# Layer 0's logits in seven tiles of 128 tokens for every eight image columns, the eighth column's weights put together by transfers

## The chip, the cores and the metric

The kernel runs on one core of a Trainium2 chip. A core has five engines that run side by side: TensorE (PE, matmuls; PEld is its weight load), VectorE (DVE), ScalarE (ACT), GpSimd (POOL) and SyncE (SP, which here only issues transfers). ACT and POOL issue transfers too. The metric is the device time of one execution in microseconds (us), and the median of several is given.

## The reference, cut to what matters

Two layers of "outlook" attention on images of 56 x 56 pixels with 384 channels, batch 8. Each layer normalises its input over groups of channels and adds its result to it. In layer 0 every pixel gets, for each of 12 heads, a 9 x 9 matrix of weights (a softmax over its last index) from its own normalised channels. These weights mix the values of its 3 x 3 neighbourhood, and the nine results are added back to the nine pixels.

```python
def _L0_conv_ref(x, Wv, Wa, Wo):             # x is normalised: _gn(x)
    v = jnp.einsum('bhwc,oc->bhwo', x, Wv)
    ...                                       # v_unf: the 3 x 3 neighbourhood of v
    a = jnp.einsum('bhwc,oc->bhwo', x, Wa).reshape(b, n, heads, k2, k2)
    attn = jax.nn.softmax(a * d ** (-0.5), axis=-1)
    out = jnp.einsum('bnhpq,bnqhd->bnphd', attn, v_unf).reshape(b, h, w, k2, c)
    ...                                       # canvas: out[..., p] added to neighbour p
    return jnp.einsum('bhwc,oc->bhwo', y, Wo)

x = x + _L0_conv_ref(_gn(x), L0_conv_Wv, L0_conv_Wa, L0_conv_Wo)
x = x + _L1_conv_ref(_gn(x), ...)             # layer 1: not touched by the change
```

## The kernel before, in words

Images go in pairs. A **column** is one image column of a pair: 2 x 56 = 112 tokens (`R`), so a pair has 56 columns (`W`) and the four pairs have 224. Layer 0 is one loop over **steps** 0 to 226 (line 802); step s attends to column s and carries older columns on behind it, so that each engine has work from several columns:

- `attend` (561): for each of three row offsets, three matmuls (`project`, each recorded twice on PE) give 288 logits for the column's 112 tokens in one of three banks of PSUM that are used in turn. DVE takes the maximum and subtracts it into the tile `at`, ACT takes the exponential. The weights of the logits are `wa_t`, the normalised input is `xn`. In seven of eight columns a tile of 128 tokens, taken across column borders, is also projected to values (`pv`, `wv_t`); ACT copies it to `v` and its queue stores it into the DRAM table `vtab0` (`spread`, 316).
- one step later `normalise` (589): DVE sums and inverts, POOL multiplies `at` by `den`.
- two steps later `presum` (602): POOL adds the weights of a column and its two neighbours into `pre`.
- three steps later `fold` (632): ACT and a small matmul with `shift` (`pw`) move rows, DVE adds into a weight tile `wt`, and ACT's queue stores it into the DRAM table `ztab0`. The weight tiles are zeroed in part by POOL before they are used again (`weights_of`, 509).

Seven columns make a **group** (`px`; seven is `PX`). Ten and eleven steps after its first column a group is loaded back: `fetch_v` (675) loads two tiles `vp` of values, `fetch` (683) two tiles `z` of weights and the residual `xres`, all on SP's queue. Four jobs `contract` (matmuls `pc`, which ACT copies to `yT`) and six jobs `project_out` (matmuls `po`, to which DVE adds `xres`) follow; they are queued with a due step, four steps after `fetch`. A step that attends has four gaps, `between(0)` to `between(3)` (813), which place the other work between its matmuls. Jobs run in gaps 0 and 2.

```python
            def between(n):

                if n == 0:
                    next(turning, None)
                    weigh()
                    jobs.run(step, 1)
                elif n == 1:
                    next(folding, None)
                    next(turning, None)
                elif n == 2:
                    jobs.run(step, 1)
                else:
                    next(folding, None)
```

So of seven steps five have jobs (remainders 1 to 5 by seven) and two have none (6 and 0). `weigh` calls `normalise` and `presum`.

The next pair's input is transposed in between (`turned`, 790), and its column blocks of four are loaded (`load`, 542) and normalised (`normed`, 550) into `xn`, which holds eight columns. `upkeep` (760) stores blocks of the first pair and fills borders of the tables with zeros, on SP's queue. The order on PE, DVE and ACT is the program's; some instructions of POOL and SP are placed by the scheduler, near their place in the program. A transfer of SP's or ACT's queue is issued in the order of its engine, so one that waits holds back what that engine has behind it.

Of the kernel before, what the change touches and what calls it, by code (L numbers as in the profile page):

```python
# [15 lines left out]
def two_outlook_layers(  # L16
# [167 lines left out]

    PH_ALL = K * HEADS0
    inside = const.tile([R, K, PH_ALL], F32, name="inside")
    gpsimd.memset(inside, 1.0)
    for b in range(IMG):
        for pi, row in ((0, b * H), (2, b * H + H - 1)):
            gpsimd.affine_select(  # L190
                out=inside[:, pi, :], in_=inside[:, pi, :], compare_op=ALU.not_equal, fill=0.0,
                base=-row, pattern=[[0, PH_ALL]], channel_multiplier=1,
            )

# [120 lines left out]

    def spread(queue, table, width, col, pad, row, v):
# [5 lines left out]
        queue.dma_start(  # L322
            bass.AP(
                table.tensor, table.offset + first,
                [[line, rows], [(R + GAP) * line - PX * C, n], [1, C]],
            ),
            v.unsqueeze(1).to_broadcast([rows, n, C]),
        )
# [73 lines left out]
    def layer0(late, pools):  # L402
# [15 lines left out]
        def xr_tile(pair, blk):  # L418
            return io.tile([P, XB, C], F32, tag="xr", name=f"xr_{pair}_{blk}")[:R]

        def stats_chunk(pair, blk, i):

            if blk == 0 and i == 0:
                stats[pair] = stat.tile([P, NCH, IMG, NBLK, 6], F32, tag="st0", name=f"st0_{pair}")
            if i == 0 and pair:
                xts[pair, blk] = block_tile("xt", pair, blk)
            xr, xt = xrs[pair, blk], xts[pair, blk]
            if pair == 0:
                pt = bank(P, 0, XB * R).rearrange("p (m r) -> p m r", m=XB)
# [12 lines left out]
            yield  # L442
# [11 lines left out]
        def blocks_in(flat, n, at=0):  # L454
# [11 lines left out]
        homes = [  # L466
            block_tile("xin", 0, 0),
            block_tile("xin", 0, 1),
            block_tile("xt", 0, 2),
            block_tile("xt", 0, 3),  # L470
            *blocks_in(first_vp[0], 2),
            *blocks_in(z_flat[1], 3),
            *blocks_in(z_flat[0], 1, NCH * NA0),
# [29 lines left out]

        wts = [fixed.tile([R, E0, HEADS0, PX], F32, name=f"wt0_{n}") for n in range(PX)]
        for wt in wts:
            vector.memset(wt, 0.0)
        held = [(0, 0)] * PX

        def weights_of(sx):

            f0, f1 = max(0, E0 - 1 - sx), min(E0, SX0 - sx)
            m0, m1 = f0 + sx - E0 + 1, f1 + sx - E0 + 1
            n = (*range(PX), 2, 3, 0, 1)[sx]
            wt = wts[n].rearrange("r e h m -> r e m h")
# [5 lines left out]
            return wts[n], wt[:, :, m0:m1, :], f0, f1  # L520

        xn = fixed.tile([P, NCH, SB, R], F32, name="xn0")

# [18 lines left out]
        def load(g):  # L542
            pair, blk = divmod(g, NBLK)
            xins[g] = io.tile([P, NCH, XB, R], F32, tag="xin", name=f"xin_{g}")
# [5 lines left out]
        def normed(g, chunks):  # L550
            scale, bias = params[g // NBLK]
            xin, to = xins[g], xn[:, :, g % 2 * XB : (g % 2 + 1) * XB, :]
            for i in chunks:
                for b in range(IMG):
                    rows = slice(b * H, (b + 1) * H)
                    scalar.activation(
                        to[:, i, :, rows], xin[:, i, :, rows], AF.Identity,
                        bias=bias[:, i, b : b + 1], scale=scale[:, i, b : b + 1],
                    )

        def attend(pair, c, between):

            nm = f"0_{pair}_{c}"
            lhs = xn[:, :, c % SB, :]
            at = work.tile([R, K, K2, PH], F32, tag="at", name=f"at_{nm}", bufs=4)
            mx = work.tile([R, K, PH], F32, tag="mx", name=f"mx_{nm}", bufs=1)
            for pi in range(K):
                pl = bank(R, BANK - NP0, BANK)
# [3 lines left out]
                vector.tensor_tensor(  # L572
                    at[:, pi], pl, mx[:, pi, :].unsqueeze(1).to_broadcast([R, K2, PH]), ALU.subtract
                )
                between(pi)
            scalar.activation(at, at, AF.Exp, scale=SCALE0)
            attns[pair, c] = at
            if c % SB:
                tile_no = c % SB - 1
                tokens = xn.rearrange("p i m r -> p i (m r)")[:, :, tile_no * P : (tile_no + 1) * P]  # L580
                pv = bank(P, 0, C)
                project(pv, tokens, wv_t, 0, C)
                v = work.tile([P, C], F32, tag="v", name=f"v_{nm}")
                scalar.copy(v, pv)
                for lo, m, row, n in parts_of(tile_no):
                    spread(scalar, vtab0, SX0, c - c % SB + m, 2, row, v[lo : lo + n])
            between(K)

        def normalise(pair, c):

            nm, at = f"0_{pair}_{c}", attns[pair, c]
            d4 = work.tile([R, K, 4, PH], F32, tag="d4", name=f"d4_{nm}", bufs=1)
# [3 lines left out]
            den = work.tile([R, K, PH], F32, tag="den", name=f"den_{nm}", bufs=1)  # L596
            vector.tensor_add(den, d4[:, :, 0], at[:, :, 8])
            vector.reciprocal(den, den)
            vector.tensor_mul(den, den, inside)
            nc.gpsimd.tensor_tensor(at, at, den.unsqueeze(2).to_broadcast([R, K, K2, PH]), ALU.mult)  # L600

        def presum(pair, c):
# [4 lines left out]
            def of(t, f, n):  # L607

                a = attns.get((pair, c + t))
                if a is None:  # L610
                    return None
                a = a.rearrange("r pi (qi qj) (pj h) -> r (pi qi) qj pj h", qj=K, pj=K)
                return a[:, :, 1 - t, f - 1 - t : f - 1 - t + n, :]
# [18 lines left out]
        def fold(pair, c):  # L632
# [5 lines left out]
            for px, sx in patches_of(c, 2):  # L638
                wt, to, f0, f1 = weights_of(sx)
                for e, pi, qi in ((0, 0, 2), (E0 - 1, 2, 0)):  # L640
                    scalar.activation(
                        to[:, e], pre[:, pi, qi, f0:f1, :], AF.Copy, scale=inside[:, qi, 0:1]
                    )
# [116 lines left out]
        def upkeep(step):  # L760

            pair, c = divmod(step, W)
            if pair == 0:

                for n in (2 * step, 2 * step + 1):
                    if n < NBLK:
                        keep_block(0, n ^ 2 if n < 4 else n)
                if c == 3:
# [14 lines left out]
            g, j = divmod(step + 2 * XB, XB)  # L783
            if j == 0 and 1 < g < NPAIR * NBLK:
                load(g)
            g, j = divmod(step + XB, XB)
            if j < NCH and g < NPAIR * NBLK:
                normed(g, (j,))

        def turned(step):  # L790
# [7 lines left out]
        vector.on = scalar.on = True  # L798
        xins.update({blk: homes[blk] for blk in range(2)})
        normed(0, range(NCH))  # L800
        LAG = 3
        for step in range(NPAIR * W + LAG):
# [3 lines left out]
            def weigh():  # L806

                if 1 <= step < NPAIR * W + 1:
                    normalise(*divmod(step - 1, W))
                if 2 <= step < NPAIR * W + 2:  # L810
                    presum(*divmod(step - 2, W))

            def between(n):
# [10 lines left out]
                else:  # L824
                    next(folding, None)

            if step < NPAIR * W:
# [346 lines left out]
```

## Time and profile before

| | |
|---|---|
| median of three runs | 3492.05 us (3486.11 to 3503.93) |
| the profiled execution: time, span | 3492.61 us, 3490.9 us |
| mean granted TensorE clock | 0.973 |
| layer 0's loop, from its first logits to its last | 62 to about 2260 us |
| logits of layer 0 on PE | 4032 matmul records, 1101.8 us busy |
| DMA, mean over the span | 240 GB/s |
| SP's queue (q1), ACT's queue (q10), POOL's (q0): share of 16 DMA engines | 48.2%, 21.2%, 7.6% |

A group of the profile is read as: line, engine, operation, what it writes and reads with the tiles' names, count, then busy time, mean nanoseconds of one, and the idle time of the engine just before, with what ended it. A "releaser" is what ended a wait. Windows give busy time of each engine between two moments, the granted clock (1.00 is full) and the share of the DMA engines that was busy. Line 118 is the helper of all matmuls, line 133 that of most other instructions.

### The profile page before, as it was taken

To read this page: it belongs to the slowest core of one execution; us is meant where nothing else is said; L and a number is where in the kernel's file an instruction comes from. 1 tells how busy PE (TensorE), PEld (TensorE's weight loads), DVE (VectorE), ACT (ScalarE), POOL (GpSimd) and SP (SyncE) were. 2 spreads that over 40 slices of the span, in tenths; PEclk is the share of its full clock that TensorE was granted. 3 is DMA by queue.
4 is the path that set the end of the run, shared out by engine and by line. 5 is a ranking of instruction groups with operands and counts; after the bars stand their busy time and mean duration, and the time that the engine had idled before them with its cause. 6 is when DMAs were issued, how large, how long until landed. Compare 5 with 4: busy or idle time off the path is not lost.

```text
span 3490.9 us, 74006 instructions
## 1 busy us (share of the span) xinstructions
PE 3315.4 (95%) x29014; PEld 2233.6 (64%) x29014; DVE 1977.1 (57%) x4797; ACT 1276.5 (37%) x3175; POOL 1258.3 (36%) x2069
## 2 busy tenths in 40 slices
PE   7897999999999999999999999978999999999997
PEld 5565666666666666666666666645666666666665
DVE  6675676767776777677777767632333323333331
ACT  4333333333333333333333333323343434343432
POOL 2543444444444444444444444522222212222220
PEclk8999999999999999999999999989999999999999
DMA  7898876868886877887766776767787787878875
GB/s 244 260 316 269 264 264 225 284 227 266 271 289 228 265 240 255 272 268 251 249 215 214 265 226 229 250 224 205 215 226 219 219 224 213 237 217 227 227 213 145
DMA packets 603259, 839.51 MB, mean 240 GB/s; under 512 B 194910, under 2 KB 496926, under 8 KB 598814
## 3 DMA queue, kind: packets, MB, share of 16 engines
q1 hardware_dynamic: 321662, 537.49, 48.2%
q10 hardware_dynamic: 253984, 210.56, 21.2%
q0 software_dynamic: 27264, 86.73, 7.6%
q8 instruction: 228, 3.74, 0.5%
q14 instruction: 121, 0.99, 0.1%
HBM read 512.95 MB, written 321.69 MB: 239 GB/s over the span
## 4 chain that ended last, share of the span: by engine, by line
PE 70%; DMA 15%; DVE 5%; issue 3%; ACT 3%; ACTq 3%; POOL 0%; SPq 0%; DVEq 0%; POOLq 0%
PE bank L118 38%; PE po L118 17%; PE pc L118 8%; DMA z<-ztab 4%; ACTq L133 3%; PE pw L118 3%; DMA at<-lgtab 2%; DMA xres<-xT 2%; DMA lgtab<-lgt 2%; ACT xn L133 2%; PE pt L121 2%; DMA ztab<-wt 1%; PE bank L121 1%; DVE mx L133 1%; DMA ztab<-zeros 1%
## 5 line engine op out<-in xcount | busy, mean ns | idle before, releaser
L118 PE MATMUL bank<-wa_t,xn 128*112 128x288 f32 x4032 | 1101.8, 411 | 13.2 <-ACT xn L133 6.6
L600 POOL TENSOR_TENSOR at<-at,den 112x972 f32<-112x972 f32 x224 | 504.4, 2252 | 1193.1 <-DVE den L133 1051.9
L118 PEld LDWEIGHTS bank<-wa_t,xn 128*112 128x112 f32 x4032 | 691.8, 178 | 297.1 <-issue 32.0
L118 PE MATMUL po<-yT,wo_t 128*128 128x448 f32 (+1 forms) x2304 | 816.4, 494 | 5.6 <-DVE x1t L133 5.1
L118 PEld LDWEIGHTS po<-yT,wo_t 128*128 128x128 f32 x2304 | 427.8, 190 | 286.9 <-issue 183.8
L133 DVE TENSOR_REDUCE mx<-bank 112x36 f32<-112x324 f32 x672 | 324.9, 484 | 431.8 <-PE bank L118 429.6
L322 POOL DMA_DIRECT2D vtab<-v x392 | 213.1, 547 | 833.1 <-DVE v L133 820.5
L133 ACT ACTIVATE at<-at 112x972 f32<-112x972 f32 (+1 forms) x256 | 243.9, 953 | 669.0 <-DVE at L133 668.9
L118 PE MATMUL bank<-wc_t,xn 128*128 128x438 f32 x1176 | 480.1, 545 | 5.7 <-issue 5.7
L118 PE MATMUL pc<-z,vp 121*32 121x49 f32 (+1 forms) x17664 | 379.9, 220 | 88.2 <-ACT yT L133 66.9
L118 PEld LDWEIGHTS pc<-z,vp 121*32 121x32 f32 (+1 forms) x17664 | 342.5, 122 | 158.2 <-ACT yT L133 88.6
L118 PE MATMUL bank<-wv_t,xn 128*128 128x384 f32 x1176 | 434.5, 507 | 0.0
L133 ACT ACTIVATE xn<-xin,bias,scale 128x224 f32<-128x224 f32 x336 | 174.1, 566 | 515.0 <-DMA ztab<-wt 210.4
L133 DVE TENSOR_TENSOR at<-bank,mx 112x324 f32<-112x324 f32 x672 | 333.0, 496 | 38.2
L118 PEld LDWEIGHTS bank<-wc_t,xn 128*128 128x128 f32 x1176 | 215.2, 192 | 176.5 <-issue 169.9
L118 PEld LDWEIGHTS bank<-wv_t,xn 128*128 128x128 f32 x1176 | 227.0, 197 | 142.4 <-issue 22.4
L622 POOL TENSOR_TENSOR pre<-at,at 112x108 f32<-112x108 f32 (+1 forms) x440 | 236.2, 537 | 58.6 <-ACT wt L133 35.9
L133 ACT COPY yT<-pc 128x294 f32<-128x294 f32 (+2 forms) x512 | 194.8, 405 | 169.8 <-PE pc L118 155.3
L133 DVE TENSOR_TENSOR lgt<-bank,ba_t 128x54 f32<-128x54 f32 x196 | 41.7, 213 | 354.5 <-PE bank L118 346.2
L133 DVE SCALAR_TENSOR_TENSOR x1t<-po,bo_t,x1t 128x448 f32<-128x448 f32 (+1 forms) x156 | 97.6, 626 | 247.3 <-PE po L118 247.3
L133 DVE RECIPROCAL den<-den 112x108 f32<-112x108 f32 (+1 forms) x256 | 198.8, 777 | 8.8
L133 ACT COPY ot<-pt 112x384 f32<-112x384 f32 x128 | 61.3, 479 | 382.4 <-PE pt L121 360.1
(106 smaller groups left out, 2913.8 us busy)
## 6 DMA issues: line engine op xcount, KB each, us to landing
z<-ztab SPq DMA_DIRECT2D x64, 2352.0 KB
vp<-vtab SPq DMA_DIRECT2D x64, 1536.0 KB
vp<-vtab SPq DMA_DIRECT2D x64, 945.0 KB
xres<-xT SPq DMA_DIRECT2D x32, 1176.0 KB
ztab<-wt ACTq DMA_DIRECT2D x336, 110.2 KB
xin<-xT ACTq DMA_DIRECT2D x54, 672.0 KB
z<-ztab SPq DMA_DIRECT2D x128, 258.4 KB
x1t<-x SPq DMA_DIRECT2D x26, 1176.0 KB
```

Source lines behind the costliest of these rows:

```text
L118: tc.keep_in_program_order(nc.tensor.matmul(*args, **kwargs))
L121: tc.keep_in_program_order(nc.tensor.transpose(*args, **kwargs))
L133: return lambda *args, **kwargs: tc.keep_in_program_order(op(*args, **kwargs))
L322: queue.dma_start(bass.AP(table.tensor, table.offset + first, [[line, rows], [(R + GAP) * line - PX * C, n], [1, C]],), v.unsqueeze(1).to_ ...
L600: nc.gpsimd.tensor_tensor(at, at, den.unsqueeze(2).to_broadcast([R, K, K2, PH]), ALU.mult)
L622: nc.gpsimd.tensor_tensor(dst, terms[0], terms[1], ALU.add)
```

## The change

The unit of `attend` becomes a tile of 128 tokens: one column (112 tokens) and 16 rows, eight of each image, of the eighth column of its group of eight (an **eighth** below). Seven such tiles cover eight columns. In the step of the eighth column (7 mod 8, a **short step** below) `attend` does nothing but call the gaps. `xn` becomes two buffers of seven tiles, normalised eight columns ahead; the odd block's last column is normalised in pieces of eight rows.

`share_out` makes the eighth column's weights, on SP's queue: the 16 rows of tiles 0 to 4 are written to the DRAM buffer `last` as each is ready; in the short step 80 rows are read back from it, and the 16 rows of tiles 5 and 6 are copied from tile to tile. `presum` and `fold` then use the result as they used a column before. The values of the 16 rows are stored with a transfer of their own. There are four weight tiles `wts` instead of seven, one buffer of `xin` instead of two, and a third job in a short step.

The core of the diff:

```diff
+    lasts = [dram.tile([R, NA0], F32, name=f"last_{n}") for n in range(2)]
+    NTILE = SB - 1
+    PART = H // NTILE
...
-        wts = [fixed.tile([R, E0, HEADS0, PX], F32, name=f"wt0_{n}") for n in range(PX)]
+        NWT = 4
+        wts = fixed.tile([P, NWT, E0 * HEADS0 * PX], F32, name="wts0")
+        xns = [fixed.tile([P, NCH, NTILE, P], F32, name=f"xn0_{n}") for n in range(2)]
...
-            n = (*range(PX), 2, 3, 0, 1)[sx]
+            n = (0, 1, 2, 3, 0, 1, 3, 2, 3, 0, 1)[sx]
...
         def attend(pair, c, between):
-            lhs = xn[:, :, c % SB, :]
-            at = work.tile([R, K, K2, PH], F32, tag="at", name=f"at_{nm}", bufs=4)
+            k, j = divmod(c, SB)
+            if j == NTILE:
+                for n in range(K + 1):
+                    between(n)
+                return
+            lhs = xns[(pair * W // SB + k) % 2][:, :, j, :]
+            at = work.tile([P, K, K2, PH], F32, tag="at", name=f"at_{nm}", bufs=4)
...
-            if c % SB:
-                tile_no = c % SB - 1
...
-                for lo, m, row, n in parts_of(tile_no):
-                    spread(scalar, vtab0, SX0, c - c % SB + m, 2, row, v[lo : lo + n])
+            spread(scalar, vtab0, SX0, c, 2, 0, v[:R])
+            end = c - j + NTILE
+            if len([*patches_of(end, 2)]) == 1:
+                spread(scalar, vtab0, SX0, end, 2, j * PART, v[R:], ((H, IMG), (1, PART)))
+            else:
+                for b in range(IMG):
+                    lo = R + b * PART
+                    spread(scalar, vtab0, SX0, end, 2, b * H + j * PART, v[lo : lo + PART])
...
+        def share_out(pair, c):
+            k, j = divmod(c, SB)
+            at, last = attns[pair, c], lasts[(pair * W // SB + k) % 2]
+            if j < NTILE - 2:
+                sync.dma_start(
+                    bass.AP(
+                        last.tensor, last.offset + j * PART * NA0,
+                        [[H * NA0, IMG], [NA0, PART], [1, NA0]],
+                    ),
+                    at[R:].rearrange("p a b c -> p (a b c)"),
+                )
+                return
+            whole = work.tile([P, K, K2, PH], F32, tag="at", name=f"at_0_{pair}_{c + 1}", bufs=4)
+            attns[pair, c + 1] = whole
+            for b in range(IMG):
+                n = b * H + (j - 1) * PART
+                sync.dma_start(
+                    whole[b * H : n].rearrange("p a b c -> p (a b c)"), last[b * H : n]
+                )
+            for t in (1, 0):
+                for b in range(IMG):
+                    n, lo = b * H + (j - t) * PART, R + b * PART
+                    sync.dma_start(whole[n : n + PART], attns[pair, c - t][lo : lo + PART])
...
             def weigh():
-                if 1 <= step < NPAIR * W + 1:
+                if 1 <= step < NPAIR * W + 1 and (step - 1) % SB < NTILE:
                     normalise(*divmod(step - 1, W))
                 if 2 <= step < NPAIR * W + 2:
+                    if (step - 2) % SB < NTILE - 2:
+                        share_out(*divmod(step - 2, W))
                     presum(*divmod(step - 2, W))
+                if step < NPAIR * W and step % SB == NTILE:
+                    share_out(*divmod(step - 1, W))
...
                 else:
                     next(folding, None)
+                    if step % SB == NTILE:
+                        jobs.run(step, 1)
```

In `load` and `normed` the buffer count and the split change as told above; in `upkeep` the calls come four columns earlier.

More of the change, by code (lines that the diff above doesn't have):

```diff
@@ L182, in two_outlook_layers, with outside @@
         gpsimd.memset(shift[:, 0, b * H - 1 : b * H], 0.0)
-    PH_ALL = K * HEADS0
-    inside = const.tile([R, K, PH_ALL], F32, name="inside")
+    NTILE = SB - 1
+    PART = H // NTILE
+    inside = const.tile([P, NTILE, K], F32, name="inside")
     gpsimd.memset(inside, 1.0)
-    for b in range(IMG):
[L189 to L193, printed above, removed]
+    def outside(j, pi, partition):
+        it = inside[:, j, pi : pi + 1]
+        gpsimd.affine_select(
+            out=it, in_=it, compare_op=ALU.not_equal, fill=0.0,
+            base=-partition, pattern=[[0, 1]], channel_multiplier=1,
+        )
+    for b in range(IMG):
+        for j in range(NTILE):
+            outside(j, 0, b * H)
+            outside(j, 2, b * H + H - 1)
+        outside(0, 0, R + b * PART)
+        outside(NTILE - 1, 2, R + b * PART + PART - 1)
     NZERO = (EP0 - E0) * ROW0
@@ L314, in parts_of, with spread @@
         yield R - done, tile_no + 1, 0, done + OVER
-    def spread(queue, table, width, col, pad, row, v):
+    def spread(queue, table, width, col, pad, row, v, rows_of=None):
         (px, sx), *more = patches_of(col, pad)
@@ L519, in weights_of @@
             held[n] = m0, m1
-            return wts[n], wt[:, :, m0:m1, :], f0, f1
-        xn = fixed.tile([P, NCH, SB, R], F32, name="xn0")
+            return weights, wt[:, :, m0:m1, :], f0, f1
         wa_t = fixed.tile([P, NCH, K * NL], F32, name="wa0_t")
@@ L587, in attend @@
-            between(K)
+            pv = bank(P, 0, C)
+            project(pv, lhs, wv_t, 0, C)
+            v = work.tile([P, C], F32, tag="v", name=f"v_{nm}")
+            scalar.copy(v, pv)
+            spread(scalar, vtab0, SX0, c, 2, 0, v[:R])
[6 more added lines that the diff above has]
+                    spread(scalar, vtab0, SX0, end, 2, b * H + j * PART, v[lo : lo + PART])
@@ L783, in upkeep @@
             g, j = divmod(step + 2 * XB, XB)
-            if j == 0 and 1 < g < NPAIR * NBLK:
-                load(g)
-            g, j = divmod(step + XB, XB)
             if j < NCH and g < NPAIR * NBLK:
                 normed(g, (j,))
+            if step < NCH:
+                normed(1, (step,), shared=False)
+            if j == NCH - 1 and 2 < g + 1 < NPAIR * NBLK and g > 2:
+                load(g + 1)
         def turned(step):
@@ L798, in layer0 @@
         vector.on = scalar.on = True
-        xins.update({blk: homes[blk] for blk in range(2)})
+        xins.update({blk: homes[blk] for blk in range(4)})
         normed(0, range(NCH))
+        normed(1, range(NCH), whole=False)
         LAG = 3
```

76 lines of the change are left out of this document (43 added, 33 removed).

## The prediction

> **What bounds the kernel now.** I read the page first: busy shares, the chain, the costliest group.
>
> ```profile
> PE 3315.4 (95%) x29014; PEld 2233.6 (64%) x29014; DVE 1977.1 (57%) x4797; ACT 1276.5 (37%) x3175; POOL 1258.3 (36%) x2069
> PE 70%; DMA 15%; DVE 5%; issue 3%; ACT 3%; ACTq 3%; POOL 0%; SPq 0%; DVEq 0%; POOLq 0%
> L118 PE MATMUL bank<-wa_t,xn 128*112 128x288 f32 x4032 | 1101.8, 411 | 13.2 <-ACT xn L133 6.6
> ```
>
> PE sets the pace, and layer 0's logits are a third of its work. But 15% of the chain is DMA, so I went on to the chain in order of time (start, us, what):
>
> ```profile
> 1032.41 18.69 DMA xres<-xT
> ...
> 1169.23 4.84 PE bank L118 x18
> ...
> 1514.52 20.22 DMA z<-ztab
> ...
> 1589.42 19.76 DMA xres<-xT
> ```
>
> One column's logits, 18 records, cost PE 4.84 us. The loads of z take 20 us. The 1.2 MB of xres take 19 us, because they are issued some 5 us after z on SP's queue and are served after it. Next SP's timeline and the windows for step 103, the kind of step that matters below:
>
> ```profile
> 1095.84 0.99 SPq L334 DMA_DIRECT2D z<-ztab  x2
> 1102.11 0.58 SPq L718 DMA_DIRECT2D xres<-xT  x1
> ```
>
> ```profile
> core 0: us, PE busy (x) PEld busy (x) DVE busy (x) ACT busy (x) POOL busy (x), PEclk, DMA share, GB/s
> 1106.00:1115.00 9.00, 6.73 (x29) 4.41 (x28) 6.88 (x18) 4.25 (x6) 3.13 (x4) 1.00 1.05 401
> 1115.00:1122.00 7.00, 6.84 (x116) 4.72 (x118) 6.01 (x15) 2.95 (x6) 5.06 (x8) 1.00 0.54 164
> 1052.40:1054.90 2.50, 0.48 (x39) 0.48 (x43) 0.80 (x3) 2.29 (x7) 2.42 (x6) 1.00 0.85 299
> 1054.90:1058.30 3.40, 3.40 (x77) 2.42 (x66) 0.77 (x2) 2.25 (x7) 1.02 (x3) 0.50 0.05 15
> ```
>
> The burst (z twice, then xres) holds the 16 DMA engines full until 1115, 19 us after its issue; by the xres row of 1032.41, whose z was issued at 1027.19, it lasts 24. The last two rows: 2 us without matmuls, then 3.4 us at half clock. Idle PE time thus costs more than itself. Two prices more, POOL's timeline of one column and the landing of a small transfer:
>
> ```profile
> 1098.64 2.25 POOL L600 TENSOR_TENSOR at<-at,den 112x972 f32<-112x972 f32 x1 [7.38 <-DVE den L133]
> 1100.97 0.41 POOL L622 TENSOR_TENSOR pre<-at,at 112x108 f32<-112x108 f32 x1
> ...
> 1102.52 0.28 POOL L620 COPY pre<-at 112x108 f32<-112x108 f32 x1
> ```
>
> ```profile
> vtab<-v POOLq DMA_DIRECT2D x56, 48.0 KB, 4.1
> ```
>
> **What goes.** Every eighth column has no logits: 28 x 4.84 = 135.5 us of PE. 128 tokens instead of 112 cost nothing: the moving side stays 288, and the values' projection, with 128 on its fixed side, takes no longer per moving column (six of 384 in 2.10 us against six of 288 in 1.62 on PE's timeline). The values' projections keep number and shape. DVE, ACT and POOL lose the softmax of 28 columns; they are not the bound, so that counts at nothing.
>
> **What moves, with nothing on the path.** Normalising x runs eight columns ahead, not four, and splits the odd block: 168 more ACTIVATEs, each under the 0.51 us of the 168-element row, against 28 exponentials of 0.95 us saved; ACT is at 37%. The load of x gets one buffer and about two steps (18 us), an eighth early; a 672 KB transfer lands in some 8 us by the chain's rows for xT (7.77, 8.45). Four weight tiles for seven raise the POOL memsets of weights from 236 to 327 (compiled order), 0.41 us each, on an engine at 36%; without that cover they would cost 91 x 0.41 = 37 us at most.
>
> **What is added.** The eighth column's weights exist only after SP has written 16 rows of tiles 0 to 4 to DRAM, read 80 rows back and copied 16 rows each of tiles 5 and 6. The compiled order shows where these stand: in the short step (7 mod 8), on SP's queue, in program order with z, vp and xres. Behind the assembly wait POOL's sum for column 6, then PE's shift of column 6 (`pw`) in the second step after, and everything PE has after that; DVE too, since the next column's buffer is the one column 5 leaves.
>
> z of a group of seven columns is issued at the start of steps 5 mod 7, and the short step passes through all seven phases. Two are bad.
>
> *Phase 5 (steps 47, 103, 159, 215):* z and xres are queued just before the assembly. With step 103's start, 1092.9, as zero: burst over at 22, transfers landed at 26 (4.1, the row above), POOL's first four sums 2 us: 28. PE meanwhile has two projections and, in three of four pairs, the matmuls of the norm (6 to 7 us), a step without jobs (three times 1.62, 2.1 for the values, 0.57: 7.5) and two thirds of the logits (3.2): it stands at 16.5. Wait 12 us, four times: 48. Ends: 0 if the queue is quicker than I read, 17 with the burst of 24 us.
>
> *Phase 6 (55, 111, 167):* z was issued one step earlier (1165.48, burst over near 1184, 13 us into step 111), but the write of tile 4's rows is queued behind it too, and the read waits for that write: 13 + 4 + 4 + 2 = 23. PE has 0.6 us in the short step, 7.5 and 5.3 in the next two, and some 3 us of wait for column 5, whose exponential, normalising (3.1 on DVE) and 2.25 on POOL lose the cover of a whole column: 16.5. Waits 3 + 6.5, three times: 28. Ends 0 and 16 each.
>
> After each of these seven waits PE runs 3.4 us or twice that at half clock and loses half of it: 7 x 2.5 = 18.
>
> *Other short steps.* Jobs that stood between logits now follow each other: in phases 3 and 4 output projections share one bank, so each waits for DVE's 0.62 us add and its start (1.5 us a step, 8 steps); phase 2 waits for ACT's copies of yT, phase 0 for column 5's chain (1.5 each, 4 steps each): 24 us, between 0 and 40.
>
> *First image pair.* The zero fills of the tables are on SP's queue too (one row of the chain is a fill of 17.55 us at 116.93; SP spends 19.43 us from 197.00 on issuing one set). Short steps 7, 15 and 23 stand behind one each: 10 + 14 + 8 = 32, between 5 and 45.
>
> *End.* Step 223's assembly stands behind the last burst but one, with nothing after it to hide it: 8, between 0 and 15.
>
> *Queue slots.* In the compiled order SP's and ACT's transfers share eight completion counters, and one waits for the transfer that had the counter before. An eighth issues 66 transfers, not 52, so ACT meets z's counter two steps after it, not three: ACT blocks earlier, while the burst sets when it goes on. ACT waits for such transfers now for 190.6 us between 300 and 2250 at its xn instructions alone, and most of that is hidden. I take 15, between -20 (its stalls merge with the seven) and 60.
>
> A page speaks against the small transfers: the Trainium skill, "DMA: Bandwidth & Descriptors", section "Why a DMA increments its semaphore by 16 and not by 1", says that a transfer is spread over the largest number of engines up to 16 that divides the slowest dimension of both sides. The write of two images by eight rows would then use two engines, its reads of 40 rows ten. No run here shows it; by it the last term would lie near its upper end and the sum near 3575, an estimate from that page. For the change speaks the Trainium skill, "Trainium Kernel Development and Optimization", "Best Practices", to tile to 128 partitions always; by that alone the sum would be 3490.9 - 135.5 = 3355.
>
> **Sum,** against the profiled execution's span: 3490.9 - 135.5 + 48 + 28 + 18 + 24 + 32 + 8 + 15 = 3528. That execution took 3492.61 for its span of 3490.9, 0.02% over the median of 3492.05, so 3530.
>
> **Rivals.** *The assembly arrives in time.* In five of seven phases nothing large is queued. If the small transfers overtook the burst, the two bad phases and their clock loss (94) would shrink to about 10, and half of the fills' term would go: 3530 - 84 - 16 = 3430, faster. It decides from a landing within 14 us of the short step's start. Against it: xres and the stores of x, issued during a burst, landed after it.
>
> *Only the long waits are real.* The small terms (24, 32, 8, 15) come to a half, 40, as jobs and logits swap places without loss: 3491, no change.
>
> *ACT falls behind.* Counters and crowded engines hold ACT past the burst, so that yT comes late in every group of seven (by the list of waits PE and its weight loads wait for ACT's yT 95 times already): 2 us more in each of 32 groups: 3594.
>
> That the change doesn't remove the work is excluded: the compiled order has seven sets of nine logits' matmuls for every eight columns.
>
> **How the numbers follow.** Forecast 0.39 (3530, by itself 3512 to 3560), in time 0.22, only the long waits 0.22, ACT behind 0.17. A difference within 0.5% (17 us) is about what a measurement of this kernel can tell from none. Faster by more is the first rival, 0.22; within 0.5% the second, 0.22; slower the forecast and the third, 0.56. The range takes both outer cases and little more: 3425 to 3600.
>
> **What would show it.** Right: `bank<-wa_t,xn` at 3528 records and some 964 us; PE gaps of about 12 us before `pw` in the second step after steps 47, 103, 159, 215, released by POOL `pre`, with SP's reads of `last` landing after xres; half clock after each. Wrong: no gap over 5 us there (first rival), or most of PE's new idle time in front of `pc` with ACT's yT as releaser (third). A PE busy time that does not fall by some 130 us would upset the first term.

## The result, and the profile after

The changed kernel takes 3746.04 us (median of four, 3740.01 to 3756.74) against 3494.16 for the kernel before in the same comparison: a ratio of 1.0723, 95% interval 1.0686 to 1.0760. The forecast was 3530, its range ended at 3600. The direction was right and the size was not.

From the page of the changed kernel: the busy line, the chain by engine, and two groups (busy, mean ns of one, idle before and what ended it).

```profile
PE 3288.0 (88%) x28510; PEld 2241.7 (60%) x28510; DVE 1837.8 (49%) x4454; ACT 1300.7 (35%) x3315; POOL 1222.6 (33%) x2160
PE 35%; DMA 9%; issue 3%; DVE 2%; ACT 2%; POOL 1%; ACTq 0%; SPq 0%; POOLq 0%; DVEq 0%
L119 PE MATMUL bank<-wa_t,xn 128*128 128x288 f32 x3528 | 999.3, 422 | 40.8 <-ACT xn L134 36.9
L119 PE MATMUL bank<-wv_t,xn 128*128 128x384 f32 x1176 | 453.0, 525 | 97.3 <-DVE at L134 97.3
```

PE fell from 95% to 88% busy. The chain accounts for little over half of the span here, so its 35% of PE can't be set beside the 70% of before; I went by the waits. The logits have the 3528 records that were foretold, but cost 422 ns each, not 411. Only 27 us of PE's 3315 went, where one eighth of the logits is 137.7: most of the rest came back as work at half clock (mean granted clock 0.931, before 0.973). The values' projection, which waited for nothing before, now waits 97 us for DVE.

The matmul records give an account of the loop of layer 0, from the first `pw` to the last, with PE's gaps over 0.15 us:

| | before | after |
|---|---|---|
| ahead of the loop | 84.3 | 90.1 |
| loop, matmuls | 2094.8 | 2062.3 |
| loop, gaps | 94.6 (51 of them) | 368.5 (102) |
| behind the loop | 1216.9 | 1223.9 |

Without the 137.7 us the matmuls would take 1957.1; they took 105 us more. By the record of the clock, matmul time at half clock in the loop is 255 us after and 87 before; half of the difference, 84 of the 105 us, is lost by it. With 274 us of new gaps and 13 us at the two ends, less the 137.7, this makes the 254 us between the spans.

The changed kernel's list of waits says where PE and DVE stop (who waits for whom, us, times, longest):

```profile
DVE at L134 <- DMA last<-at: 148.1, 19, 12.6
PE bank L119 <- DVE at L134: 100.0, 15, 9.9
PE pc L119 <- ACT yT L134: 97.0, 40, 11.7
PE pw L119 <- POOL pre L677: 73.4, 10, 14.9
```

Two timelines show two of these waits. First SP in step 103 and PE in step 105, where a long wait was foretold, with the windows around it (columns as in the windows of the prediction):

```profile
1218.92 2.90 SPq L134 DMA_DIRECT2D at<-last  x2
1222.67 10.63 SPq L134 DMA_DIRECT2D at<-at  x4
```

```profile
1236.34 1.14 PE L119 MATMUL pw<-pre,shift 112*112 112x120 f32 x4 [9.03 <-POOL pre L677]
```

```profile
1227.30:1236.30 9.00, 0.01 (x1) 0.00 (x0) 2.50 (x6) 0.00 (x0) 1.14 (x4) 0.64 0.77 292
1236.30:1239.70 3.40, 3.36 (x10) 2.65 (x11) 1.92 (x5) 1.57 (x4) 2.72 (x3) 0.50 0.24 59
```

SP needs 10.63 us to get the four copies out; POOL's sum and `pw` follow. PE does nothing for 9 us (first row of the windows: 0.01 us of PE) and then runs 3.4 us at half clock (0.50). In the compiled order the first of these copies takes the completion counter that a load of z had, and the last the one that xres had: SP issues them only when those have landed (at 1222.61 and 1232.65 in the trace). Second, step 77 (PE):

```profile
922.04 1.63 PE L119 MATMUL bank<-wa_t,xn 128*128 128x288 f32 x6
933.25 3.69 PE L119 MATMUL bank<-wv_t,xn 128*128 128x384 f32 x6 [9.58 <-DVE at L134]
```

No assembly stands here. An early write of 16 rows, issued at 921.26 after z (906.73) and xres (912.14, itself held until 918.6) on SP's queue, lands at 932.58, when they are through: the last packet of xres starts at 931.2, and those of the write run from 930.5 to 931.9. Until then its tile `at` is not free, DVE can't subtract into it, and PE has no bank. The prediction priced these writes at nothing.

### The profile page after: what moved, and what is told of

Read it like the earlier page. It is cut to its first block, busy times and chain, and to the rows that moved or that the text cites. A ratio compares the mean times of both kernels' runs of the same rounds, so it can differ in the third digit from the quotient of the medians.

```text
span 3745.1 us, 73661 instructions
## 1 busy us (share of the span) xinstructions
PE 3288.0 (88%) x28510; PEld 2241.7 (60%) x28510; DVE 1837.8 (49%) x4454; ACT 1300.7 (35%) x3315; POOL 1222.6 (33%) x2160
## 3 DMA queue, kind: packets, MB, share of 16 engines
q1 hardware_dynamic: 328774, 558.40, 46.8%
## 4 chain that ended last, share of the span: by engine, by line
PE 35%; DMA 9%; issue 3%; DVE 2%; ACT 2%; POOL 1%; ACTq 0%; SPq 0%; POOLq 0%; DVEq 0%
PE bank L119 17%; PE po L119 10%; PE pc L119 5%; DMA at<-lgtab 2%; DMA lgtab<-lgt 2%; PE pw L119 1%; DMA z<-ztab 1%; ACT xn L134 1%; DMA last<-at 1%; DMA vtab<-v 1%; PE pt L122 1%; PE bank L122 1%; DMA xres<-xT 1%; DVE den L134 0%; DVE mx L134 0%
## 5 line engine op out<-in xcount | busy, mean ns | idle before, releaser
L119 PE MATMUL bank<-wa_t,xn 128*128 128x288 f32 x3528 | 999.3, 422 | 40.8 <-ACT xn L134 36.9
L119 PE MATMUL po<-yT,wo_t 128*128 128x448 f32 (+1 forms) x2304 | 836.4, 503 | 40.3 <-DVE x1t L134 37.7
L119 PEld LDWEIGHTS bank<-wa_t,xn 128*128 128x128 f32 x3528 | 672.7, 198 | 265.8 <-ACT xn L134 34.0
L134 POOL TENSOR_TENSOR at<-at,den 128x972 f32<-128x972 f32 x196 | 441.2, 2251 | 1122.9 <-DVE den L134 658.2
L134 DVE TENSOR_REDUCE mx<-bank 128x36 f32<-128x324 f32 x588 | 285.7, 486 | 447.3 <-PE bank L119 444.8
L134 ACT ACTIVATE at<-at 128x972 f32<-128x972 f32 (+1 forms) x228 | 215.5, 945 | 645.5 <-DVE at L134 645.4
L134 ACT ACTIVATE xn<-xin,bias,scale 128x168 f32<-128x168 f32 (+1 forms) x474 | 208.3, 502 | 621.8 <-DMA ztab<-wts 261.9
L134 DVE TENSOR_TENSOR at<-bank,mx 128x324 f32<-128x324 f32 x588 | 291.5, 496 | 222.9 <-DMA last<-at 148.1
L134 ACT ACTIVATE wts<-pre,inside 112x48 f32<-112x48 f32 (+4 forms) x672 | 180.1, 359 | 83.1 <-POOL wts L134 18.2
L119 PE MATMUL pw<-pre,shift 112*112 112x120 f32 x896 | 135.7, 275 | 73.4 <-POOL pre L677 73.4
```

Of the source, the lines that this page charges most:

```text
L119: tc.keep_in_program_order(nc.tensor.matmul(*args, **kwargs))
L134: return lambda *args, **kwargs: tc.keep_in_program_order(op(*args, **kwargs))
```

## The experiments

The first theory was read from these rows. *Early writes*: tiles `at` held by writes behind the burst. Its rivals were *late assembly*, *short steps* (jobs in a row) and *counters* (ACT held because SP's and ACT's transfers share eight completion counters). Ratios are against the kernel before, run beside each group; 1% is 35 us. "Transfers" are those on the shared counters per eighth in the compiled order: 52 before, 66 after.

**No transfers in `share_out`.**

```diff
         def share_out(pair, c):
...
+            attns[pair, c + 1] = at
+            return
```

> Leaves out all transfers of share_out: the eighth column uses column 6's weights, so nothing is written to last, read back or copied. It shows what the short step is worth without its transfers. Theory 'early writes' (the writes of the 16 rows of tiles 0 to 4 stand behind z and xres on SP's queue, keep their tile at from being reused, and so stop DVE and PE) and theory 'late assembly' (the reads and copies in the short step come late, as predicted) both expect that nearly all of the new idle time goes with them: 3490.9 - 135.5 + about 30 for the short steps' back-to-back jobs = 3370 to 3410 us, granted clock back to 0.97. Theory 'short steps' (the jobs without logits between them, ACT and the counters are the cost) expects at least 3550 us, with the waits in front of pc as large as in the changed kernel (97 us).

1.0171 (1.0156 to 1.0186), 3556 us, 55 transfers. Three quarters of the loss went (193 of 252 us), but both theories about `share_out` missed the time: without any of its transfers, and with the logits gone, the kernel is still slower than before. PE's gaps are 207 us. This run's timelines show one at work; SP, then ACT, then PE:

```profile
845.94 0.99 SPq L347 DMA_DIRECT2D z<-ztab  x2
```

```profile
861.58 0.94 ACTq L134 DMA_DIRECT2D vtab<-v  x2
868.43 0.81 ACTq L134 DMA_DIRECT2D ztab<-wts  x2
869.29 1.59 ACT L134 ACTIVATE xn<-xin,bias,scale 128x168 f32<-128x168 f32 x4 [9.17 <-DMA vtab<-v]
870.79 0.51 ACT L134 COPY xt<-pt 128x448 f32<-128x448 f32 x1
```

```profile
871.35 1.01 PE L122 MATMUL pt<-ident,xr 112*128 112x112 f32 x4 [5.07 <-ACT xt L134]
```

By the compiled order the store of `wts` at 868.43 takes the counter that the second load of z had. ACT can't issue it until z has landed, at 868.36, 22 us after its issue (the row of `xn` names a store instead, but ACT waited for z's counter until 868.36), and nothing behind it on ACT runs: not `xn`, not the copy `xt`, for which PE stands 5 us.

**Only the early writes elsewhere**: `sync.dma_start` becomes `gpsimd.dma_start` (POOL's queue), or `scalar.dma_start` (ACT's), for the write to `last`.

> Only the five early writes of an eighth go to POOL's queue; the reads and copies stay on SP's. 'Early writes': the waits of DVE for last<-at (148 us) and of PE for DVE at bank<-wv_t (97 us) go, with half-clock time that follows them: 3746 - 148 - some 60 = 3520 to 3580 us; what is left is the assembly's gaps before pw in steps 48, 104, 160, 216 (10 to 15 us each). 'Late assembly': the time falls by under 60 us (above 3690), since the gaps before pw and behind them are the loss and the writes only waited beside it.

> Only the five early writes go to ACT's queue, whose transfers are small (24 to 110 KB). 'Early writes': as with POOL's queue, 3520 to 3580 us. If ACT is held by its issues and by the completion counters it shares with SP (a rival of the prediction: ACT falls behind), 140 more issues on it cost more than the waits they take away, and the time stays above 3700 with more idle time of PE in front of pc and wa_t, released by ACT.

POOL: 1.0595 (1.0574 to 1.0616), 61 transfers. ACT: 1.0685 (1.0665 to 1.0705), 66 transfers. On POOL's queue DVE's wait of 148 us for `last` is gone from the list, and yet the gain is 45 us, about a quarter of what "early writes" expected; on ACT's it is 13, within the intervals.

**All of `share_out` on POOL's queue** (writes, reads and copies).

> All transfers of share_out go to POOL's queue, none stays behind z and xres. 'Early writes' together with 'late assembly' expect 3430 to 3500 us: both kinds of waits go, and POOL pays for issuing 11 transfers per eighth (308 of about 1 us) on an engine that is 33% busy, and for waiting for the landings of tile 4's write. If instead the 16 DMA engines themselves are full (the order on the queue not being the cause), the gaps in steps 0 mod 7 and before pw stay and the time is above 3650.

1.0426 (1.0400 to 1.0453), 55 transfers: 104 us better than the change, but far from the 3430 to 3500 of the two theories together. POOL's issues of these transfers took 0.50 to 0.62 us each, not the 1 us of the expectation.

**The values' 16-row stores on POOL's queue**, on top of the kernel without transfers in `share_out`.

```diff
-                spread(scalar, vtab0, SX0, end, 2, j * PART, v[R:], ((H, IMG), (1, PART)))
+                spread(gpsimd, vtab0, SX0, end, 2, j * PART, v[R:], ((H, IMG), (1, PART)))
```

> As the kernel without transfers in share_out (3556 us; the eighth column uses column 6's weights), and the values' 16-row stores go to POOL's queue, so that ACT issues one store of values a step, not two or three, and shares fewer of the eight completion counters with z and xres. Theory 'counters' (ACT is held because its small transfers wait for the counters of z and xres): ACT meets those counters a step later, and half or more of the 101 us that PE waits longer for ACT go, with their half clock: 3430 to 3490 us. Theory 'cover' (the burst of z and xres holds ACT and the DMA engines equally long as before, and PE, with 135 us less to do, now arrives before it is over): 3530 to 3570.

0.9967 (0.9953 to 0.9981), 45 transfers: 71 us better for moving ten stores of 24 KB per eighth off ACT. "Counters" had it.

**The change's layout with the work left in**, and a shorter burst in both kernels.

```diff
-            if j == NTILE:
-                for n in range(K + 1):
-                    between(n)
-                return
-            lhs = xns[(pair * W // SB + k) % 2][:, :, j, :]
+            lhs = xns[(pair * W // SB + k) % 2][:, :, min(j, NTILE - 1), :]
```

> As the kernel without transfers in share_out, but the eighth step does a column's full logits and softmax again (on tile 6's tokens, so its output leaves the eighth column's right weights out), without the third job in that step: the change's layout (tiles of 128, four weight tiles, one xin buffer, stores of 16 rows) without its removed work. 'Cover' and 'short steps': the removed work's 135.5 us come back but the waits it uncovered go, so 3490 to 3530, and the removal is then worth less than zero. If the changed layout itself costs (fewer weight tiles and buffers, more ACTIVATEs, more stores): 3600 to 3690.

> As the kernel without transfers in share_out, and xres is loaded once, not 32 times (later groups add the first group's residual): a third of each burst is gone, from 4.7 to 3.5 MB with vp. 'Cover': ACT's holds end some 6 us earlier in each of 32 groups and most of what PE waits for goes: 3400 to 3440 us. 'Short steps' (jobs that follow each other without logits between them): the time falls by under 40 us, to 3520 or more.

> The kernel before, with xres loaded once: the control for the run with the shorter burst. 'Cover' says that here the burst is hidden: under 40 us faster (3450 to 3490). If the burst costs the kernel before as much as the changed one, it falls by over 80 us, and the burst is no reason for the difference between the two.

Full eighth: 1.0136 (1.0113 to 1.0160). So with all stores on ACT, taking out the logits (1.0136 to 1.0171) gained nothing: the kernel was 12 us slower, with intervals that just touch. Without xres: 1.0102 (1.0075 to 1.0129) from 1.0171, and the kernel before 0.9943 (0.9922 to 0.9965). Both gain about the same, 24 and 20 us. xres is 1.2 of the 6.0 MB of z and xres (384 packets of 3136 bytes, 2048 of 2352), a fifth of the burst, not the third of the expectation. As far as that fifth goes, the length of the burst is no reason for the difference; "cover", as I had put it, fell.

**Counters, in four kernels**: complete with `share_out` and the 16-row stores on POOL; the full eighth with those stores on POOL; the kernel before with the second of its two stores on POOL; and the kernel before with tiny transfers that nothing needs:

```diff
+            if c % SB != SB - 1:
+                for n in range(2):
+                    row = 2 * (pair * W + c) + n
+                    sync.dma_start(tiny[row : row + 1], ident[n : n + 1, :64])
```

> Nothing left out: all transfers of share_out and the values' 16-row stores on POOL's queue. 'Counters' expects that what the values' stores cost without transfers in share_out (73 us) goes here too: 3648 - 73 = 3550 to 3590 us. If POOL, with 22 transfers to issue per eighth, becomes the engine that PE waits for (pre before pw): 3620 or more.

> As the run with a full eighth step (3541 us; the eighth column's right weights are left out), with the values' 16-row stores on POOL's queue. 'Counters': the layout's 47 us over the kernel before are these stores and go: 3480 to 3505. If four weight tiles, one xin buffer and the split normalising are the cost: 3525 to 3545.

> The kernel before with the second of its two stores of values per tile on POOL's queue, so that ACT and SP share the counters among 45 transfers per eighth, not 52. 'Counters' with holds that are hidden in the kernel before: within 20 us of 3494. If ACT's holds cost the kernel before as they cost the changed one: 3420 to 3450.

> The kernel before, with 14 transfers of 256 bytes per eighth more on SP's queue (two a step in seven of eight steps), which nothing reads: 66 transfers per eighth, as in the changed kernel. ACT issues none of them. 'Counters': ACT meets the counters of z and xres, and of tiny transfers queued behind them, earlier and is held longer: 3560 to 3640 us, PE's waits for ACT (yT, xt, xn) 80 us or more above those of the kernel before. If only ACT's own issues or the bytes matter: 3490 to 3510.

Complete on POOL: 1.0143 (1.0113 to 1.0172), 45 transfers, a little better than "counters" expected. Full eighth: 0.9982 (0.9962 to 1.0002), 45. Before, second store on POOL: 0.9921 (0.9905 to 0.9937), 45; by ratio these 27 us lie between its two expectations, so the counters cost the kernel before too, but less than the changed one. Before with tiny transfers: 1.0206 (1.0183 to 1.0230), 66. The last is the clearest: 14 transfers of 256 bytes per eighth, which ACT doesn't issue and nobody waits for, cost the kernel before 72 us, 0.18 us each. That takes ACT's own issues and the bytes out of the question. From the `pw` of column 28 to the last one, ACT's idle time that a transfer ended is 460 us, where the kernel before has 381: ACT is held longer, about as much as the kernel loses. That the tiny transfers delay SP's own issues as well is not excluded. PE's gaps grew by 46 us in all, not by the 80 expected of its waits for ACT. Two rows of the lists of waits, first of the kernel before, then with the tiny transfers:

```profile
PE pc L118 <- ACT yT L133: 66.9, 35, 7.8
ACT xn L133 <- DMA vtab<-v: 91.3, 21, 10.3
```

```profile
PE pc L119 <- ACT yT L134: 97.9, 37, 7.6
ACT xn L134 <- DMA vtab<-v: 119.3, 26, 10.1
```

**The early writes again**: as the run with them on POOL's queue, with a tiny transfer on SP's queue in the place of each.

```diff
+                row = pair * W + c
+                sync.dma_start(tiny[row : row + 1], ident[:1, :64])
```

> As the run with the early writes on POOL's queue (1.060), and in the place of each write, on SP's queue, a transfer of 256 bytes that reads a constant: as many transfers on the eight counters as in the changed kernel, at the same places, but no tile at is held by them. 'Early writes' (the tile at that waits for its write is the loss): 1.055 to 1.065, as without them. 'Counters' (the writes cost by their number on the counters): 1.068 to 1.080, back at the changed kernel's 1.072, with PE waiting for ACT in place of DVE.

1.0698 (1.0664 to 1.0731), 66 transfers: dummies that keep only the number on the counters and SP's issues bring 36 of the 45 us back, and what is left, some 9 us, is within the intervals. No tile `at` is held by a write here; the waits moved (in the changed kernel these three are 97.0, 73.4 and 25.3):

```profile
PE pc L120 <- ACT yT L135: 117.0, 45, 10.3
PE pw L120 <- POOL pre L680: 100.6, 14, 14.8
PE pt L123 <- ACT xt L135: 60.1, 17, 7.4
```

My first theory named a wait that was really there, 148 us in all, and was wrong on what it cost: the wait of DVE covered waits for ACT and POOL that came out when it went.

**No job in a short step**, without transfers in `share_out` and in the complete kernel (both with small transfers on POOL).

```diff
                     weigh()
-                    jobs.run(step, 1)
+                    if step % SB != NTILE:
+                        jobs.run(step, 1)
```

> As the run without transfers in share_out and with the values' 16-row stores on POOL (0.997 of the kernel before; the eighth column uses column 6's weights), with no contract or project_out job in a short step: they wait for the next step's gaps, where logits stand between them. Theory 'jobs in a row' (what eats the removed 135 us is that pc and po follow each other in the short step and wait for ACT's yT and DVE's add, with half clock behind each wait): the gaps at pc and po fall from 102 us to about 55, the time to 0.96 to 0.98 of the kernel before. Theory 'ACT and DMA pace' (the short step only shows a group that is paced by its transfers): the gaps move to other steps and the time stays at 0.99 to 1.01.

> Nothing left out: all transfers of share_out and the 16-row stores on POOL (1.014 of the kernel before), and no job in a short step. 'Jobs in a row': 0.975 to 0.995; the assembly, which has POOL wait 17 us for its copies, keeps some of it. 'ACT and DMA pace', or an assembly that loses the cover of the short step's jobs: 1.01 to 1.03.

0.9953 (0.9936 to 0.9969) from 0.9967, and 1.0172 (1.0152 to 1.0191) from 1.0143. "Jobs in a row" fell: a gain of 5 us and a loss of 10, both within the intervals. The gaps moved. With jobs in the short step (list of waits, then PE's timeline and ACT's in step 79):

```profile
PE pc L119 <- ACT yT L134: 91.3, 39, 9.4
PE bank L119 <- ACT xn L134: 23.7, 7, 6.1
```

```profile
862.60 0.66 PE L119 MATMUL pw<-pre,shift 112*112 112x120 f32 x4
867.05 2.19 PE L119 MATMUL pc<-z,vp 121*32 121x49 f32 x96 [3.79 <-ACT yT L134]
869.76 4.46 PE L119 MATMUL po<-yT,wo_t 128*128 128x448 f32 x6 [0.52 <-ACT yT L134]
```

```profile
863.95 1.59 ACT L134 ACTIVATE xn<-xin,bias,scale 128x168 f32<-128x168 f32 x4 [2.53 <-DMA vtab<-v]
866.16 0.53 ACT L134 COPY xt<-pt 128x448 f32<-128x448 f32 x1 [0.62 <-ACT xn L134]
866.59 0.72 ACT L134 COPY yT<-pc 128x294 f32<-128x294 f32 x2
```

and without them:

```profile
PE bank L119 <- ACT xn L134: 80.3, 24, 6.6
PE pc L119 <- ACT yT L134: 32.6, 24, 5.1
```

While PE stands for `yT`, ACT normalises `xn` and copies `xt`, which come first in its order. Without jobs PE is through the short step at once and waits in front of the next column's logits, for the `xn` that ACT has not normalised yet. Either way it meets ACT.

**All stores of values on POOL's queue**: in the kernel before, in the complete changed kernel (with `share_out` there too), and in the latter without `share_out`'s transfers.

```diff
-            spread(scalar, vtab0, SX0, c, 2, 0, v[:R])
+            spread(gpsimd, vtab0, SX0, c, 2, 0, v[:R])
```

> The kernel before with both stores of values per tile on POOL's queue (the run with one of them there: 0.992). 'Counters': 38 transfers per eighth share them in place of 45, a further gain of up to the first one's: 0.980 to 0.992. If POOL's issues (some 1 us each) now delay its sums, and so pw: 0.995 to 1.02.

> Nothing left out: the changed kernel with all transfers of share_out and all stores of values on POOL's queue, so that no transfer of the change and none of the values is on the counters that ACT shares with SP (with the values' 112 rows still on ACT: 1.014 of the kernel before). If ACT's holds are what eats the removed logits: 0.985 to 1.005. If the assembly (pw gaps of 33 us, POOL waiting for its copies) is what is left: 1.010 to 1.025. It is to be set beside the kernel before with all values on POOL, 0.983.

> As the run just named, but without transfers in share_out (the eighth column uses column 6's weights): the ceiling of the change with ACT as free of counters as this study gets it. If ACT's holds ate the removed logits, the removal is now worth something against the kernel before with all values on POOL (0.983): 0.950 to 0.972. If PE in the short step catches up with ACT's own order of work, holds or not: 0.975 to 0.990.

Before: 0.9826 (0.9804 to 0.9848). Changed, complete: 1.0041 (1.0021 to 1.0061). Without `share_out`'s transfers: 0.9815 (0.9790 to 0.9840). All have 38 transfers. The second lies at the end of the range given for ACT's holds, the third in the range for ACT's own order of work, which the expectation set against it. The first is the fastest complete kernel of this study, 61 us below the kernel before; it owes nothing to the change. The third equals it, though PE has 137 us less to do. Its account against the first: matmuls 1985.9 to 2074.6, so 49 of the 137 us came back (31 of them by matmul time at half clock, 103 us to 42; mean clock 0.966 to 0.978), and gaps 127.7 to 46.4. The list of waits of the first,

```profile
PE pc L118 <- ACT yT L133: 30.2, 18, 5.2
```

and of the third:

```profile
PE pc L119 <- ACT yT L134: 61.4, 30, 5.8
PE po L119 <- DVE x1t L134: 23.8, 27, 2.5
PE bank L119 <- ACT xn L134: 21.9, 7, 10.4
```

So ACT's holds are not what eats the removed logits: ACT's idle time that a transfer ended, counted as above, is 146 us in the first and 89 in the third. With few holds PE still runs into results that ACT and DVE have not delivered. In the third's loop ACT ends 31 of PE's gaps, 68 us in all; during them ACT was at work for 50 us, 30 of these at `xn`, and idle for a transfer for 5. Without `share_out`'s transfers but with all stores on ACT it was idle for a transfer in 58 of 154 us of such gaps, in the complete change in 70 of 145. So with few holds PE waits for ACT's work in its order; no kernel with another order on ACT was run, so what that would bring is open.

Runs by their number of transfers (those with all jobs in place and xres loaded each time):

| transfers per eighth | kernel before | full eighth | no transfers in `share_out` | complete change |
|---|---|---|---|---|
| 66 | 1.0206 (tiny) | | | 1.0723; writes on ACT's queue 1.0685; dummies for writes 1.0698 |
| 61 | | | | 1.0595 |
| 55 | | 1.0136 | 1.0171 | 1.0426 |
| 52 | 1.0000 | | | |
| 45 | 0.9921 | 0.9982 | 0.9967 | 1.0143 |
| 38 | 0.9826 | | 0.9815 | 1.0041 |

Down each column the time falls with the number: 0.11 to 0.15% per transfer in the kernel before, 0.15 to 0.28% in the complete change, where the steps down to 55 also take transfers from behind z and xres on SP's queue. Across a row, the column without transfers is never clearly below those to its left.

## Why the prediction was wrong, step by step

*What goes, -135.5 us: the step that failed first.* The records went as foretold, but "PE sets the pace" was used as if every microsecond of PE counted in full. Measured by putting the logits back: +12 us (55 transfers) and -5 us (45) for the removal, -4 against the kernel before at 38. The prediction's own sign against this term came: PE's busy time fell by 27 us, not 130. PE's 95% hid that ACT and DVE follow it closely: where PE has a step's work less, they are late, as the counts of ACT's work above show for 38 transfers.

*Queue slots, 15 us: the step that failed by most.* The mechanism was named and mis-sized. Fourteen more transfers cost 72 us even in the kernel before. In the complete change the fall from 66 to 38 is worth 6.8%, where the kernel before gains 1.7% from 52 to 38: the difference, 5.1%, is 178 us; it holds the number on the counters and, for the writes, reads and copies, their place behind z and xres, which only the run with dummies took apart. The reason given for a small term, that most of ACT's waits "is hidden", did not hold for further ones. The rival "ACT falls behind" had the right engine, and with 3594 two fifths of the size, but not the place: of 274 us of new gaps 25 are in front of `pc`.

*The long waits, 48 + 28 us: the first right in place and size, the second in size alone.* Gaps before `pw` in steps 49, 105, 161 and 217 are 10.3, 9.0, 12.6 and 14.9, together 46.8. In phase 6 the step after the short one (56, 112, 168) has a gap of 2.7 to 2.8 in its first logits, for ACT's `xn`, and one of 8.7, 7.4 and 7.5 in front of the values' projection; together they are 31.9. The first is no part of the assembly: without `share_out`'s transfers it is there with the same 2.7 to 2.8. The second is DVE waiting for the tile that the write of tile 4's rows holds, not the sum in front of `pw`. So the 28 came out by luck. That the copies wait for counters of z and xres, more than for their turn on the queue, was not foretold. What the assembly costs in all, with few transfers on the counters, is 0.9815 to 1.0041, 79 us.

*Half clock, 18 us: mis-sized.* It was counted behind seven waits. There are 57 gaps over 2 us after, 16 before, and half clock cost 84 us more. In step 79 of the run above, a wait of 3.79 us is followed by `pc` at 2.19 us and `po` at 4.46, where others of the same count took 1.45 and 2.43 a few us before and after.

*Other short steps, 24 us: too small.* Gaps at `po` grew by 35 us, at `pc` by 25, at the logits by 25, at `pt` by 25. At 38 transfers, with no assembly, the gaps of the whole loop are 81 us above those of the kernel before at the same number, and the matmuls 49 above what the removal would leave. Single ones reach 4 to 6 us, not 1.5.

*Fills, 32 us:* the first 28 steps have 67 us of gaps, 27 before; but 47 of them stay without `share_out`'s transfers, so about 20 belong to the assembly. *End, 8:* right. The gap before the `pw` of column 222, which step 223's assembly holds, is 11.8 us, before 4.5: 7.4.

*Early writes, priced at nothing:* 36 of their 45 us are their number on the counters, and the tile they hold is worth 9 or nothing while the counters are as they are.

In ratios, the removal with its layout is -4 us (at 38 transfers), the assembly +79, the counters and what they hold +178, together 253. That they add up to the whole is no proof: they are differences of the same ratios. The two pages weighed in the prediction: the Trainium skill, "DMA: Bandwidth & Descriptors", section "Why a DMA increments its semaphore by 16 and not by 1", agrees with the packets: the 16 of an early write (3888 bytes, 152 ns each) run as two rows of eight, one packet after the other in each, over 1.4 us at 930.5. So the write takes little over one microsecond, which is not what decided. The Trainium skill, "Trainium Kernel Development and Optimization", section "Best Practices", with its 128 partitions, stood for 3355 in the prediction; no kernel here got anything clear of the noise from the fuller tiles (0.9815 against 0.9826).

## What to carry to other kernels

A share of 95% for one engine does not say that removing its work pays: ask who delivers next, and put the work back on top of the change before believing in the removal. Count the transfers that share completion counters, as one counts bytes: an engine whose next transfer needs the counter of a load in a large burst stands until that has landed (22 us above), and moving small stores to a queue with other counters was worth more here (61 us) than an eighth of the logits. A wait that the list puts at 148 us may be worth next to nothing: replace its cause by a dummy that keeps everything else.

## What was not expected of the hardware

A transfer of 256 bytes that nothing reads costs 0.18 us of the kernel's time (14 x 28 of them, 72 us), while ACT, which issues none of them, is held 79 us longer by transfers. And a gap costs more than its own length: 274 us of new gaps brought 84 us of half clock with them, and in one case 3.79 us without matmuls were followed by 2.8 us lost at the lower clock (0.74 at `pc`, 2.03 at `po`).
